# A chain of four convolution layers on one core: queues of the stores, steps of the division, layout of x2, place of the weight preparation

## The chip, the cores and the metric

The kernel runs on one core of a Trainium2 chip. Its engines are TensorE (PE, matrix products; PEld is its weight load), VectorE (DVE), ScalarE (ACT), GpSimd (POOL) and SyncE (SP, which here only issues DMAs). Each engine works through its own instructions in order and waits on semaphores where it needs another's result. Sixteen DMA engines carry the transfers, which are issued from SP's queue and from ACT's. The metric is the device time of one execution in microseconds (us), as the median of several runs.

## The reference

Four layers on x of 4 images, 128 x 128 pixels, 128 channels, all in float32. Before each layer stands a group normalisation over 32 groups of four channels (`_gn`), and each layer's output is added to its input.

```python
# layer 0: deformable convolution (offsets from a 1x1 product), relu
x = x + relu(deform_conv(gn(x), ...))
# layer 1: a scan over image rows; conv1d of width 9 along a row
def step(carry, row):
    new = row + relu(conv1d_same(carry, W));  return new, new
# layer 2: each pixel, the sum over its row and the sum over its column
x = x + (v @ Wself.T + (v.sum(2) @ Wm.T)[:, :, None] + (v.sum(1) @ Wk.T)[:, None]),  v = gn(x)
# layer 3: triangle multiplication
xn = layer_norm(gn(x))
left, right = (xn @ left_w) * sigmoid(xn @ lgate_w), (xn @ right_w) * sigmoid(xn @ rgate_w)
out = einsum('bkjd,bkid->bijd', left, right)
x = x + (layer_norm(out) * sigmoid(xn @ ogate_w)) @ to_out_w
```

(The biases and the gains of the norms are left out here; the kernel has them.)

## The kernel before

The kernel is one program with four stages one after the other.

`deform_layer` (layer 0) takes the first 3083 us and is not touched by the change. It leaves x1 in DRAM.

`last_weights` (L1158) and `message_weights` (L1225) prepare the weights of the last layers: the four projection matrices and the gate matrix are loaded (ACT's queue; the biases on SP's), scaled by the norm's gain, and brought into the form `wcat` by PE products of 512 and 128 columns, whose results go through two PSUM banks of their own and are copied by DVE. This stands between layer 0 and layer 1.

`scan_layer` (layer 1, L1011) goes row by row over all four images at once, 128 rows. SP loads four rows of x1 at a time (`x1rows`), PE transposes each row (`x1T_ps`), ACT applies the norm (`rowT`), and PE computes the convolution of the row before in two halves (`both_ps`, `own_ps`, three banks for the latter), which DVE adds up (`total`, `carry`). The rows of x2 are collected four at a time in `x2c`; DVE takes their statistics and their sums, and ACT's queue stores them to `x2T` in DRAM, split into a left and a right half of each row (two stores per image, L1148). A scheduler decides the order of the instructions in this stage.

`message_terms` computes the sums of layer 2 that are the same along a row or a column.

`last_layers` (L1289) does layers 2 and 3 image by image. Here the order on every engine is the one in which the program writes it (`manual_schedule`); generators are advanced step by step in a loop at the end of the function, so that the work of two images interleaves:

- `messages(b)`: 16 steps. SP loads 16 half rows of x2 (`x2c`, L1348), two steps ahead; PE multiplies (L1364); DVE adds `zc`, which POOL made, and writes X (L1369), an SBUF array of the whole image with the channels on the partitions; DVE takes two statistics (L1374).
- `scaled(b)`: 3 steps. The statistics become the norm's scale by a short chain DVE, PE (L1387), DVE, PE (L1398), ACT (`s`, L1400), DVE, PE (L1410). Ahead of `s` in the program stand eight stores of X to `x3T` in DRAM, 1 MB each, on SP's queue (L1395).
- `normed(b)`: 25 steps. PE centres X in tiles of eight columns (L1456); ACT squares (`sq`, L1462); ACT and DVE in turn write the centred tile back to X (L1467, L1469); for each group of two tiles PE sums the squares over the channels (L1490). Each group then starts a `divided` generator.
- `divided(b, j0, pv)`: ACT takes the square root (`std`, L1421). The 2048 values lie along one row, so they go through DRAM: SP stores them (L1424), loads them spread over the partitions (`rstd`, L1427), DVE takes the reciprocal (L1429), SP stores it (L1431) and loads it copied to all partitions (`rwide`, two loads of 256 KB for each half group, L1437), and X is multiplied by it (L1445), one of the two parts on DVE and one on POOL. Each of these lies one step behind the other, the multiplication two. The divisions that aren't finished when `normed` ends are advanced in the next stage.
- `multiplied(b, q)`: for each quarter q of the hidden channels 16 steps of projections (PE L1515, ACT sigmoid `sig` L1520, DVE product into T L1523), with the gates' product every second step (`gate`, stored to `gateT` from SP), then 8 steps of products over pixels (L1542). In the last quarter the messages of the next image run beside it.
- `given_out(b)`: 32 output columns of four, with six steps of lead for the statistics (L1567): layer norm (`u`, by ACT and POOL), transposes (L1601), `y` (ACT, then POOL times `gate`), and the products with x3 and the output weights (L1612, L1616); SP loads x3 and the gate and stores the output. It runs beside the next image's stages; for the last image it runs alone.

The tiles `std`, `rwide` and `sig` take turns in one set of four buffers (tag `half`); `gate` has three of its own; `x2c`, `zc` and `sq` share four (`wide`). A tile that takes a buffer waits until the last user of it is done.

## Time and profile before

| | |
|---|---|
| median of 3 runs | 5491.95 us (5491.25 to 5511.62) |
| profiled execution | 5500.92 us, its span 5499.1 us, mean granted clock 0.956 |
| PE busy | 4923.4 us, 90% of the span |
| DVE, ACT, POOL busy | 3263.9, 2492.0, 1269.4 us |
| layer 0 | to 3083 us |
| preparation of weights | 3083 to 3106.5 us |
| scan | 3106.5 to 3966.7 us |
| terms of the messages | to 3986.3 us |
| first image: first message product, first centring product, first projection | 3986.3, 4044.9, 4102.0 us |
| second image, the same | 4265.2, 4357.4, 4418.1 us |
| third image, the same | 4632.7, 4724.9, 4784.7 us |
| fourth image, the same | 4999.2, 5091.4, 5151.4 us |
| last output alone | 5390 to 5499.1 us |

Times within the span are counted from its start. A line of the timeline gives the start, the length, the engine ("q" for its queue of DMA issues), the line of the kernel, the operation, what it writes and reads, and in brackets how long the engine had been idle before it and what ended that. A line of the view of waits gives who waited for whom, how long in total, how often, and the longest in us. A line of the view by stage gives the stretch and its length, and for each engine its busy time and, in brackets, its number of instructions, in the order PE, PEld, DVE, ACT, POOL; then the granted clock of PE, the share of the DMA engines and what they moved in GB/s.

### The profile page before, as it was taken

To read this page: it belongs to the slowest core of one execution; us is meant where nothing else is said; L and a number is where in the kernel's file an instruction comes from. 1 tells how busy PE (TensorE), PEld (TensorE's weight loads), DVE (VectorE), ACT (ScalarE), POOL (GpSimd) and SP (SyncE) were. 2 spreads that over 40 slices of the span, in tenths; PEclk is the share of its full clock that TensorE was granted. 3 is DMA by queue.
4 is the path that set the end of the run, shared out by engine and by line. 5 is a ranking of instruction groups with operands and counts; after the bars stand their busy time and mean duration, and the time that the engine had idled before them with its cause. 6 is when DMAs were issued, how large, how long until landed. Compare 5 with 4: busy or idle time off the path is not lost. (4 is left out here: it accounts for less than half of the span.)

```text
span 5499.1 us, 163068 instructions
## 1 busy us (share of the span) xinstructions
PE 4923.4 (90%) x68902; PEld 4257.7 (77%) x68902; DVE 3263.9 (59%) x8405; ACT 2492.0 (45%) x5131; POOL 1269.4 (23%) x1161
## 2 busy tenths in 40 slices
PE   1898899999999998989999799999979789798897
PEld 1787788888888787878899699999838478486596
DVE  4676666666566656665555466666654655556445
ACT  1555454544554544545544133222224465564565
POOL 4222221210221201212000011111240343333424
PEclk9999999999998999999999899999989999899998
DMA  4776656665566765655544233333251544545436
GB/s 150 162 161 150 128 135 145 145 150 100 136 140 138 158 120 110 150 115 135 119 94 86 74 82 78 78 78 78 58 172 59 191 157 135 189 154 187 150 131 194
DMA packets 1390555, 710.69 MB, mean 129 GB/s; under 512 B 978765, under 2 KB 1245294, under 8 KB 1380598
## 3 DMA queue, kind: packets, MB, share of 16 engines
q1 hardware_dynamic: 1243538, 658.56, 47.6%
q10 hardware_dynamic: 146276, 41.60, 3.4%
q8 instruction: 545, 8.93, 0.7%
q14 instruction: 196, 1.61, 0.1%
HBM read 417.28 MB, written 282.55 MB: 127 GB/s over the span
## 5 line engine op out<-in xcount | busy, mean ns | idle before, releaser
L606 PE MATMUL conv_ps<-ring,wdef 128*128 128x192 f32 (+2 forms) x7632 | 1304.3, 320 | 7.1 <-DVE x1c L576 5.0
L514 DVE TENSOR_TENSOR m<-t_ps,tent 128x390 f32<-128x390 f32 x1548 | 806.7, 557 | 784.5 <-ACT tent L512 769.0
L606 PEld LDWEIGHTS conv_ps<-ring,wdef 128*128 128x128 f32 x7632 | 1150.0, 196 | 127.7 <-issue 64.8
L512 ACT COPY tent<-t_ps 128x390 f32<-128x390 f32 x1560 | 691.2, 488 | 654.6 <-PE t_ps L498 646.0
L498 PE MATMUL t_ps<-parts_of,spread 57*64 57x99 bf16 (+1 forms) x12384 | 743.1, 275 | 167.5 <-DVE m L514 146.8
L523 PE MATMUL v_ps<-m,pixels 60*64 60x108 f32 (+1 forms) x22704 | 811.6, 264 | 20.8 <-DVE m L514 8.7
L498 PEld LDWEIGHTS <-spread 57*64 57x64 bf16 x12480 | 578.8, 126 | 313.2 <-issue 265.8
L523 PEld LDWEIGHTS v_ps<-m,pixels 60*64 60x64 f32 x22704 | 672.0, 137 | 71.4 <-DVE m L514 21.3
L549 ACT COPY ring<-v_ps 128x432 f32<-128x432 f32 x1032 | 505.6, 525 | 452.1 <-PE v_ps L523 451.3
L420 POOL TENSOR_TENSOR off<-off,koff 72x512 f32<-72x512 f32 x128 | 162.9, 1273 | 1770.2 <-DVE off L417 1770.2
L1515 PEld LDWEIGHTS pair_ps<-wcat,X 128*128 128x128 f32 x4096 | 486.7, 196 | 79.5 <-issue 65.5
L1515 PE MATMUL pair_ps<-wcat,X 128*128 128x128 f32 x4096 | 498.0, 280 | 34.7 <-DVE T L1523 28.9
L1523 DVE TENSOR_TENSOR T<-pair_ps,sig 128x256 f32<-128x256 f32 x512 | 281.1, 592 | 389.0 <-ACT sig L1520 388.1
L1110 PEld LDWEIGHTS own_ps<-diff,wconv 128*128 128x128 f32 x4064 | 493.6, 191 | 13.1
L1110 PE MATMUL own_ps<-diff,wconv 128*128 128x128 f32 x4064 | 494.6, 273 | 0.0
L506 PE MATMUL t_ps<-parts_of,spread 57*64 57x130 bf16 x9288 | 455.1, 225 | 0.0
L1153 POOL TENSOR_TENSOR sum_h<-sum_h,x2c 128x512 f32<-128x512 f32 x128 | 162.7, 1271 | 1162.7 <-DVE x2c L1136 1162.7
L438 DVE SCALAR_TENSOR_TENSOR parts<-off,parts 72x512 bf16<-72x512 f32 x384 | 296.3, 772 | 152.5 <-ACT parts L430 146.8
L506 PEld LDWEIGHTS <-spread 57*64 57x64 bf16 x9312 | 319.3, 108 | 0.1
L1068 ACT ACTIVATE rowT<-x1T_ps,t_x,s_x 128x128 f32<-128x128 f32 x512 | 200.9, 573 | 248.6 <-PE x1T_ps L1064 232.0
L1520 ACT ACTIVATE sig<-pair_ps 128x512 f32<-128x512 f32 x256 | 151.8, 597 | 332.2 <-PE pair_ps L1515 190.4
L1099 PE MATMUL both_ps<-carry,wsum 128*128 128x128 f32 x2032 | 270.5, 275 | 6.0 <-DVE carry L1133 1.4
(197 smaller groups left out, 6736.9 us busy)
## 6 DMA issues: line engine op xcount, KB each, us to landing
pixels<-tab SPq DMA_DIRECT2D x688, 123.8 KB
parts_of<-off SPq DMA_DIRECT2D x1032, 55.7 KB
off<-parts SPq DMA_DIRECT2D x64, 891.0 KB
tab<-rows SPq DMA_DIRECT2D x384, 128.0 KB
xin<-in_x_dram SPq DMA_DIRECT2D x128, 256.0 KB
x<-x1c SPq DMA_DIRECT2D x32, 1024.0 KB
x1rows<-x SPq DMA_DIRECT2D x128, 256.0 KB
x2T<-x2c ACTq DMA_DIRECT2D x256, 128.0 KB
```

The costliest lines, as they stand in the source:

```text
L438: nc.vector.scalar_tensor_tensor(parts[:, NSPLIT + i, h : h + RO, 2 : S + 2], off, 0.0, part, ALU.is_gt, ALU.mult,)
L498: nc.tensor.matmul(tp[h : h + HALF, 0, 0:n].rearrange("p (r c) -> p r c", c=PADW)[:, :, i:PADW:RX], lhsT=spread[0:k, kx // 2, i, h : h + H ...
L506: nc.tensor.matmul(tp[h : h + HALF, 1, i * PADW : (i + 1) * PADW], lhsT=spread[HALF : HALF + k, kx // 2, first + i, h : h + HALF], rhs=src ...
L512: nc.scalar.copy(tent[:, 0:n], tp[:, 0, 0:n])
L514: nc.vector.tensor_tensor(m, *pair, ALU.mult)
L523: nc.tensor.matmul(to[p1 : p1 + HALF], lhsT=pix[p0 : p0 + LANES, xb, :], rhs=m[p0 : p0 + LANES, :, RX * xb : RX * xb + w], start=True, sto ...
L549: nc.scalar.copy(to, bodies[side])
L606: nc.tensor.matmul(pc[:, at : at + rows, x0:x1], lhsT=wdef[:, side, k, :], rhs=v[:, :, k if v.shape[2] == NK else kx, x0 + kx : x1 + kx], ...
L1099: nc.tensor.matmul(both, lhsT=wsum[:, j, :], rhs=old[h][:, 1, :, j : j + V], start=(j == 0), stop=(j == NJ - 1),)
L1110: nc.tensor.matmul(own[:, n], lhsT=wt[:, 2 * j + n, :], rhs=diffs[h][:, n, :, j : j + V], start=False, stop=(n == 1 and j == NJ - 1),)
L1515: nc.tensor.matmul(pj[:, j], lhsT=X[:, j0 + j, :], rhs=w.wcat[:, q * 4 * DQ : (q + 1) * 4 * DQ], start=True, stop=True,)
L1523: nc.vector.tensor_tensor(to, pj[:, :, e].rearrange("p j d -> p d j"), sig[:, :, e].rearrange("p j d -> p d j"), ALU.mult,)
```

## The change

- The preparation of the weights is called from within the scan, at row 8, and takes its PSUM banks from the scan's `own_ps`.
- x2T is laid out in whole rows: one store per image and four rows in place of two; a load of the messages takes half of each of 16 rows, in pieces of 256 bytes.
- The eight stores of x3T are issued from ACT's queue.
- `std` takes a buffer of the gates' three, `sig` and `rwide` have two each; both parts of the multiplication are on DVE; in `divided` there are two steps between the issue of a transfer of the std and its use, and one in place of two between the loads of `rwide` and the multiplication.
- `given_out` has seven steps of lead in place of six, and its steps are spread otherwise over the stages of the next image.

```diff
@@ scan_layer
+            if y == 2 * RB:
+                beside(ps_y, "own_ps")
...
-                    for n in range(2):
-                        nc.scalar.dma_start(
-                            x2T[b, :, n, y0 : y + 1, :], x2c[:, b, :, n * V : (n + 1) * V]
-                        )
+                    nc.scalar.dma_start(x2T[b, :, y0 : y + 1, :], x2c[:, b])
@@ last_weights
-            pw = ps_w.tile([P, 512], F32, name="prep_ps")
+            pw = psum.tile([P, 512], F32, name="prep_ps", tag=bank)
...
-            pb = ps_w.tile([P, 512], F32, name="prepb_ps")
+            pb = psum.tile([P, 512], F32, name="prepb_ps", tag=bank)
@@ messages
-                    nc.sync.dma_start(x2c, x2T[b, :, n, y0 : y0 + RB, :])
+                    nc.sync.dma_start(
+                        x2c, x2T[b, :, y0 : y0 + RB, n * V : (n + 1) * V]
+                    )
@@ scaled
-                nc.sync.dma_start(x3T[b, :, j0 : j0 + 16, :], X[:, j0 : j0 + 16, :])
+                nc.scalar.dma_start(x3T[b, :, j0 : j0 + 16, :], X[:, j0 : j0 + 16, :])
@@ divided
-            std = four.tile([P, 512], F32, name="std", tag="half")
+            std = three.tile([P, 512], F32, name="std", tag="gate")
             nc.scalar.activation(std, pv, AF.Sqrt, bias=c.eps)
...
             nc.sync.dma_start(stdT[b, 0, tokens].rearrange("(q e) -> q e", q=4), std[0:P:32])
             yield
+            yield
             rs = two.tile([P, 2 * JB], F32, name="rstd")
             nc.sync.dma_start(rs, stdT[b, 0, tokens].rearrange("(p e) -> p e", p=P))
             yield
+            yield
             nc.vector.reciprocal(rs, rs)
             yield
             nc.sync.dma_start(stdT[b, 1, tokens].rearrange("(p e) -> p e", p=P), rs)
+            yield
             yield
             for h in range(2):
                 rws = []
                 for j1 in (j0 + h * JB, j0 + h * JB + 4):
-                    rw = four.tile([P, 4 * S], F32, name="rwide", tag="half")
+                    rw = two.tile([P, 4 * S], F32, name="rwide")
...
                 yield
-                yield
-                for (j1, rw), engine in zip(rws, (nc.vector, nc.gpsimd)):
+                for j1, rw in rws:
                     flat = X[:, j1 : j1 + 4, :].rearrange("p j i -> p (j i)")
-                    engine.tensor_tensor(flat, flat, rw, ALU.mult)
+                    nc.vector.tensor_tensor(flat, flat, rw, ALU.mult)
@@ multiplied
-                sig = four.tile([P, JB, 2 * DQ], F32, name="sig", tag="half")
+                sig = two.tile([P, JB, 2 * DQ], F32, name="sig")
@@ given_out
-            for k in range(-6, NS_ + 1):
+            for k in range(-7, NS_ + 1):
...
-                if k + 6 < NS_:
-                    statistics(k + 6)
-                    if k + 7 in groups:
-                        scales(groups[k + 7], k + 7)
+                if k + 7 < NS_:
+                    statistics(k + 7)
+                    if k + 8 in groups:
+                        scales(groups[k + 8], k + 8)
@@ last_layers, the loop over images
-            n = 0
-            while step(msgs):
-                step(out_of, 2 if n < 2 else 1)
-                n += 1
-            for _ in scaled(b):
-                step(out_of)
+            step(out_of)
+            for n, _ in enumerate(msgs):
+                if n < 3:
+                    step(out_of)
+            for n, _ in enumerate(scaled(b)):
+                step(out_of, (2, 1, 1)[n])
             norm = normed(b)
             for n in range(25):
                 step(norm)
-                if n in (7, 15, 23):
+                if n in (4, 9, 14, 19, 24):
                     step(out_of)
@@ tile_preact_convs
-    x2T = dram.tile([B, P, 2, S, S // 2], F32, name="x2T")
+    x2T = dram.tile([B, P, S, S], F32, name="x2T")
...
-    w = last_weights(tc, c, wp, w3)
     with tc.tile_pool(name="l2", bufs=1) as l2:
-        w2 = message_weights(tc, l2, (wself_T, wm_T, wk_T))
-        counted = scan_layer(tc, c, l2, x1, w_conv, norms, x2T)
+        made = []
+
+        def weights(psum, bank):
+            made.append(last_weights(tc, c, wp, w3, psum, bank))
+            made.append(message_weights(tc, l2, (wself_T, wm_T, wk_T)))
+
+        counted = scan_layer(tc, c, l2, x1, w_conv, norms, x2T, weights)
+        w, w2 = made
```

More of the change, by code (lines that the diff above doesn't have):

```diff
@@ L1008, in deform_general, with scan_layer @@
                 nc.vector.tensor_copy(to, v)
-def scan_layer(tc, c, small, x1, w, norms, x2T):
+def scan_layer(tc, c, small, x1, w, norms, x2T, beside):
     nc = tc.nc
@@ L1155, in scan_layer, with last_weights @@
     return stats, sum_w, sum_h
-def last_weights(tc, c, wp, w3):
+def last_weights(tc, c, wp, w3, psum, bank):
     nc = tc.nc
@@ L1185, in last_weights @@
     w.gcols = slice(NQ * 4 * DQ, NP_)
-    with tc.tile_pool(name="l3prep", bufs=1) as prep, tc.tile_pool(
-        name="l3ps_w", bufs=2, space=PSUM
-    ) as ps_w:
+    with tc.tile_pool(name="l3prep", bufs=1) as prep:
         raw = prep.tile([P, NP_], F32, name="wraw")
```

## The prediction

> **What bounds the kernel now.** I read the page first, then the busy time by stage, then who waits for whom, then the timeline of the stages in which TensorE (PE) idles.
>
> ```profile
> span 5499.1 us, 163068 instructions
> ...
> PE 4923.4 (90%) x68902; PEld 4257.7 (77%) x68902; DVE 3263.9 (59%) x8405; ACT 2492.0 (45%) x5131; POOL 1269.4 (23%) x1161
> ```
>
> PE is busy 90% of the span, so a change that leaves the products alone can gain at most the 576 us in which PE idles. Only stages from 3083 us on are touched. The view by stage (busy us per engine, granted clock, DMA share, GB/s):
>
> ```profile
> 3083.00:3106.50 23.50, 4.51 (x8) 2.26 (x8) 4.96 (x16) 0.00 (x0) 0.00 (x0) 0.52 0.65 147
> 3106.50:3966.70 860.20, 854.06 (x7116) 834.03 (x7116) 567.87 (x1433) 257.64 (x766) 161.47 (x127) 1.00 0.31 76
> 4680.70:4709.10 28.40, 13.55 (x37) 6.62 (x36) 27.65 (x54) 8.42 (x16) 10.17 (x6) 0.83 0.80 282
> 4709.10:4725.00 15.90, 11.38 (x55) 10.09 (x56) 7.01 (x28) 9.54 (x19) 3.57 (x3) 0.71 0.97 379
> 4725.00:4784.70 59.70, 48.49 (x178) 18.94 (x177) 18.16 (x34) 37.70 (x48) 20.41 (x19) 0.90 0.38 116
> ```
>
> Row 1 is the preparation of weights between deformation and scan: PE does 4.5 us of work in 23.5. Row 2 is the scan: PE 99% busy, so nothing that relieves DVE, ACT or a queue there can gain. Rows 3 to 5 are the third image's last five message steps (DVE busy 27.7 of 28.4, so DVE bounds), `scaled` (PE waits on a chain, and the DMA engines are 97% busy) and `normed` (no engine full: PE 48.5 of 59.7). From the waits:
>
> ```profile
> POOL X L1445 <- DMA rwide<-stdT: 93.0, 36, 31.6
> ACT std L1421 <- POOL X L1445: 54.1, 14, 7.1
> ```
>
> and the third image's timeline:
>
> ```profile
> 4694.08 13.88 SPq L1395 DMA_DIRECT2D x3T<-X  x8
> ...
> 4761.44 0.69 ACT L1421 ACTIVATE std<-one_ps,eps 128x512 f32<-128x512 f32 x1 [5.08 <-POOL X L1445]
> ...
> 4770.64 1.92 PE L1490 MATMUL one_ps<-sq,mean 128*32 128x512 f32 x4 [8.84 <-ACT sq L1462]
> ...
> 4797.61 5.79 PE L1515 MATMUL pair_ps<-wcat,X 128*128 128x128 f32 x32 [4.99 <-DVE T L1523]
> ```
>
> `std`, `rwide` and `sig` share four buffers. ScalarE's `std` waits until a division (POOL, L1445) frees one; ACT's next squares stand behind it; PE's variance product waits 8.84 us for those, and the projections 4.99 us for a `sig` held the same way. What sets the pace is the division loop, seen undisturbed in the first image:
>
> ```profile
> 4079.86 0.79 SPq L1437 DMA_DIRECT2D rwide<-stdT  x2
> ...
> 4081.18 4.45 SPq L1437 DMA_DIRECT2D rwide<-stdT  x2
> ...
> 4084.02 1.27 POOL L1445 TENSOR_TENSOR X<-X,rwide 128x512 f32<-128x512 f32 x1 [1.97 <-PE one_ps L1490]
> ...
> 4088.42 1.27 POOL L1445 TENSOR_TENSOR X<-X,rwide 128x512 f32<-128x512 f32 x1 [1.23 <-DMA rwide<-stdT]
> 4088.52 0.79 SPq L1437 DMA_DIRECT2D rwide<-stdT  x2
> ```
>
> Two round trips of `rwide` per group of 16 columns, 4079.86 to 4088.52: 8.7 us a group, where PE and ACT alone take 4.7 (the first three `std` start at 4055.3, 4060.0, 4064.6).
>
> **The change, part by part.** Savings are counted against the profiled execution (span 5499.1, time 5500.9); the median of the runs, 5492.0, is 8.9 lower, and I take the same saving off it.
>
> *Start of the scan.* Its first transposes start at 3106.56, after the weights' copies (the idle before them ends with DVE `wcat`). Now the loads of x1 come first on SP, from 3089.4, where the first bias load was; four issues take 1.8 us. No row shows their landing; the nearest is the last weight load, issued 3096.54 and used by PE at 3101.0: 4.5 us. So PE starts near 3095.7: -10.9. The preparation moves into row 8 of the full scan: two products of 512 columns at 1.0 (two of that size take 1.98 us in the message stage) and two of 128 at 0.27 = 2.5 us of PE. They take `own_ps` banks, of which there are three; the instruction order puts a 2.27 us `sum_w` between two of the four copies on DVE, and PE's next `own_ps` is behind: between 0 and 5 us, I take 2. DVE's 2.5 us hide in its free third. Sum -6.4, bounds -3 and -10.
>
> *x2 in whole rows.* Four stores in place of eight per four rows, on an ACT that has 70% free beside a full PE: nothing, and about the same for the last stores, since PE idles there for DVE's statistics. The loads (L1348) now read 256 bytes at a time, 2048 pieces a load. Nearest row: ACT's queue, which carries the x2 stores in such pieces, took 3.4% of 16 engines for 146,276 packets, 20.4 ns each, so 2.6 us a load over 16 engines; as now laid out, 512 KB at the first image's 210 GB/s at share 0.64 (328 at full) take 1.6. So +1.0 a load. DVE paces these steps at 3.12 us and each load is issued two steps ahead: hidden, except for a few tenths at the start, where PE already waits for loads (0.7 to 1.9 us a step): +2 in the first image, +1 in each other. If every step waited: +14 and +3.
>
> *x3T stores from ACT.* SP no longer stands 13.9 us over them; the loads of `gate` and x3 behind no longer make PE wait (1.26 and 1.66 us, image 3). The eight issues, 0.3 to 0.85 us each on SP, now stand ahead of `u` and of `s` on ACT. The last four wait for the last X; DVE then needs 3.6 us to L1387 and 1.4 more to L1398 before `s`, and four issues at 0.55 plus `u` at 2.1 fit into 5.0. Cover gone, they cost up to 4. [...] I take nothing, because in the changed program's list of waits the stores wait for the DMA eight places earlier, which are those loads; the first image's first store waits for all of them. The same holds the other way: the first `rstd` load waits for the fifth store to land. Four stores after the last X are 4 MB, 12.8 us at 328 GB/s, down some 15 us after it; the first `std` comes 3.6 + 8.5 + 9 = 21 us after it: hidden by 6 us, and each us beyond that would delay the first division by one.
>
> *Steps of the output moved.* Before: 7 in the messages, 3 in `scaled`, 3 in `normed`, 26 in the projections; now 4, 4, 5, 27 with one more step of lead. DVE's message steps lose three statistics at 1.2: -3.6, and the loads' +1 makes -2.6. `scaled` now meets steps -3 to 0, of which PE works only in the last two: 3.6 us (the first image, with no steps: 4041.35 to 4044.94) + 1.1 + 1.1 of transposes + 1.7 of products + 1 waiting for the first y = 8.5 for 15.8: -7 (bounds -3, -9). The extra step in the projections costs a full 1.9.
>
> *Buffers and steps of the std.* `std` goes to the gates' three buffers, `sig` and `rwide` get two each, and both multiplications go to DVE at 0.68. ACT's waits for POOL are gone. What is late next is DVE: it stands in order at each multiplication until `rwide` lands, and its X (L1469) and T (L1523) are behind. Loop with two buffers: a pair lands about 4.1 us after the first issue, two multiplications, next issues as each buffer comes free: 4.0 to 4.5 a trip, two trips, 8.0 to 9.0 a group; I take 8.7. But PE may run a group ahead. From the first centring product: `std` at 9.0, then 7.0 where an output step stands between (4.7 + 2.3) and 4.7 where not; the first multiplication, three groups behind, at 27, the fifth at 27 + 4 x 8.7 = 62. PE reaches the projections at 53 (before 59.7), does two steps, and waits for T behind that fifth multiplication until 62.5; before, it resumed at 4797.6 - 4725.0 = 72.7. So -10, with two more output steps inside. Later waits of 1 us: -1.
>
> *Sum.* Images 2 to 4: -2.6 - 7 - 10 + 1.9 - 1 = -18.7 each, -56. First image, no output steps: the third projection step resumes at 58 for 66.4 (4111.35), half of its later waits of 1.9 and 1.2 gone, loads +2: -8. Last output: one more statistics step of 1.2 ahead of the first y: +1.5; its 3 us stalls (PE for `u`) stay, since the square root stands in the same place in ACT's order. With the start: -69. Median 5492 - 69 = **5423**.
>
> **Rivals.**
> *PE runs through (0.16).* The trips shorten to about 3.3 us, since less stands on SP. For: the single trip 4085.3 to 4088.4 took 3.1. Against: both trips carry two loads. Then `normed` and start give -15, `scaled` -9, messages -4, an image -29; the first -13; start -9: 5383.
> *The loop stays long (0.12).* SP's queue also holds output stores, gate loads that wait for POOL, and `std` stores, and two buffers leave no slack: 12 us a group. The fifth multiplication comes at 75, -10 becomes +3, an image -6, the first +2: 5471.
> *Slower, by the same loop (0.10).* DVE must do all multiplications in order, so past 12.7 us a group the T behind the seventh and eighth groups is late too: at 14, +11 in the start of the projections and +9 further on, an image +11, the first +15: about 5535. For: one step, about 2 us, between load and use, where there were two. Against: the present trips.
> *The change does not do what it says:* the stores of x3 gain nothing from their own queue because the DMA engines are 97% busy in `scaled`; its -7 becomes -3: 5435, inside the forecast.
>
> **How the numbers follow.** Forecast 0.62, its own range 5387 to 5460 from the bounds above. A measurement of this kernel tells about 0.5% from no change, 5464.5 to 5519.4. Faster: 0.61 of the forecast, 0.16, and 0.04 of the long loop: 0.81; same: 0.10 (mostly the long loop); slower 0.09. The range reaches into the run-through case below and over the long loop above: 5375 to 5482.
>
> **What would show it.** Right: no `std` waiting for POOL; PE's wait for squares in `normed` under 2 us; L1364 to L1387 about 25 us in image 3, then 8 to 9 to the first centring product; DVE waiting for `rwide` some 2 us twice a group, and PE waiting for T once per image by 2 to 4 us; the scan's first transposes 11 us earlier after 3083. Wrong: multiplications of successive groups 11 us apart or more; PE waiting for x2 loads in every message step; `s` in `scaled` ended by ACT rather than PE.

## The result, and the profile after

The changed kernel takes 5459.34 us, the median of five runs (5454.3 to 5471.3), where the kernel before takes 5492.53 us over five (5491.25 to 5511.62). The ratio is 0.9935, with a 95% interval of 0.9915 to 0.9956: faster by 0.65%. The forecast was 5423 us (range 5375 to 5482), a gain of 69 us; 33 us came.

The page of the changed kernel, from an execution of 5471.3 us, the longest of its five runs:

```profile
span 5469.6 us, 162747 instructions
...
PE 4908.4 (90%) x68902; PEld 4255.7 (78%) x68902; DVE 3298.1 (60%) x8469; ACT 2491.3 (46%) x5131; POOL 1192.2 (22%) x1097
```

PE is still busy 90% of the span. The view by stage, with the stages and columns in the order of the prediction (start of the scan, scan, last message steps of the third image, `scaled`, `normed`):

```profile
3078.10:3090.90 12.80, 0.02 (x1) 0.05 (x1) 3.13 (x12) 0.00 (x0) 0.00 (x0) 0.50 0.42 114
3090.90:3945.80 854.90, 852.75 (x7124) 836.67 (x7124) 578.00 (x1436) 259.93 (x766) 161.41 (x127) 1.00 0.26 80
4657.60:4686.00 28.40, 13.31 (x28) 4.81 (x27) 26.26 (x44) 2.23 (x4) 9.24 (x5) 0.82 0.84 252
4686.00:4695.80 9.80, 7.79 (x26) 5.52 (x27) 7.58 (x31) 7.27 (x15) 2.54 (x2) 0.50 1.02 422
4695.80:4758.40 62.60, 51.72 (x210) 22.87 (x209) 27.77 (x52) 45.12 (x63) 12.59 (x12) 0.92 0.45 144
```

The start takes 12.8 us where it took 23.5 us, and `scaled` 9.8 for 15.9. The third row begins at the end of the last product of T (4657.6); from that point the messages took 32.1 us before (4677.0 to 4709.1), so that they are 3.8 us shorter, although the prediction's row, which begins later, has the same 28.4 us. The scan is 5.3 us shorter, which the forecast did not have. `normed` is *longer*, 62.6 for 59.7, where a good part of the gain was to come from. The timeline of the changed kernel at the end of that stage (in brackets the idle time and what ended it):

```profile
4739.38 1.34 DVE L1446 TENSOR_TENSOR X<-X,rwide 128x512 f32<-128x512 f32 x2 [2.50 <-DMA rwide<-stdT]
...
4743.31 1.29 DVE L1446 TENSOR_TENSOR X<-X,rwide 128x512 f32<-128x512 f32 x2 [1.39 <-DMA rwide<-stdT]
...
4747.44 0.31 ACT L1585 ACTIVATE rs<-rs,eps 128x16 f32<-128x16 f32 x1 [9.76 <-DVE rs L1582]
...
4751.26 1.92 PE L1491 MATMUL one_ps<-sq,mean 128*32 128x512 f32 x4 [7.29 <-ACT sq L1463]
...
4758.86 1.32 DVE L1446 TENSOR_TENSOR X<-X,rwide 128x512 f32<-128x512 f32 x2 [2.40 <-DMA rwide<-stdT]
...
4763.05 1.28 DVE L1446 TENSOR_TENSOR X<-X,rwide 128x512 f32<-128x512 f32 x2
4764.25 1.10 DVE L1524 TENSOR_TENSOR T<-pair_ps,sig 128x256 f32<-128x256 f32 x2
```

No `std` waits for POOL any more. In its place ACT stands 9.76 us at `rs`, the square root of an *output* step that lies among the normalisation's tiles. It waits for DVE, which takes that step's statistics in order behind two pairs of multiplications, each held up by its `rwide`. ACT's next squares stand behind the root, and PE waits 7.29 us for them.

Stage by stage, the two profiled executions set against the forecast, in us. A row with two numbers gives the length of the stage before and after the change; the scan is counted here to the first product behind it, 8.1 us after its own last one:

| step of the forecast | forecast | measured |
|---|---|---|
| layer 0, same code (end of its last product at 3066.4, 3061.5) | 0 | -4.9 |
| from there to the scan's first transposes: 40.2, 29.4 | -10.9 | -10.8 |
| the scan with the preparation in it: 868.2, 863.0 | +4.5 | -5.2 |
| first image, messages: 55.1, 69.9 | +2 | +14.9 |
| first image, `normed` and first quarter of the projections | -10 | -5.2 |
| images 2 to 4, messages | -7.8 | -10.8 |
| images 2 to 4, `scaled` | -21 | -18.6 |
| images 2 to 4, first centring product to third projection step | -30 | -7.9 |
| images 2 to 4, rest of the projections | +2.7 | +10.5 |
| last output: 102.1, 110.6 | +1.5 | +8.5 |
| sum | -69 | -29.5 (span) |

The rows are differences of points in time read from the two traces. The rest of the projections holds the extra output step in the last quarter (+5.9, forecast +5.7).

### The profile page after: what moved, and what is told of

It is laid out like the page before. It is cut to its first block, busy times and chain, and to the rows that moved or that the text cites. A ratio compares the mean times of both kernels' runs of the same rounds, so it can differ in the third digit from the quotient of the medians.

```text
span 5469.6 us, 162747 instructions
## 1 busy us (share of the span) xinstructions
PE 4908.4 (90%) x68902; PEld 4255.7 (78%) x68902; DVE 3298.1 (60%) x8469; ACT 2491.3 (46%) x5131; POOL 1192.2 (22%) x1097
```

## The experiments

My theory after the result had four parts: in the first image the loads of x2 are late (small pieces, or the stores beside them); in images 2 to 4 two limits hold `normed`, the output's square root on ACT and the loop of `rwide`; the granted clock, 0.75 over 82.1 us of the last output, makes that longer; and the scan gained from something in the stores of x2. Each run below edits the changed kernel. "Ratio" is that of its time to the kernel before, with a 95% interval; lengths of stages are those of its one profiled execution.

**x2 laid out as before.**

```diff
-                    nc.scalar.dma_start(x2T[b, :, y0 : y + 1, :], x2c[:, b])
+                    for n in range(2):
+                        nc.scalar.dma_start(
+                            x2T[b, :, n, y0 : y + 1, :], x2c[:, b, :, n * V : (n + 1) * V]
+                        )
...
-                    nc.sync.dma_start(
-                        x2c, x2T[b, :, y0 : y0 + RB, n * V : (n + 1) * V]
-                    )
+                    nc.sync.dma_start(x2c, x2T[b, :, n, y0 : y0 + RB, :])
...
```

> The changed kernel with x2 laid out as before: eight stores of half rows per four rows, loads of 4 KB in one piece per partition. Theory (the 256-byte pieces make the first image's message steps wait for their loads): the stretch from the first message product to the first product of the scale falls from 69.9 us to about 55 us, and PE's wait for x2c there from 26 us to about 5 us; the time falls by 10 to 15 us. Rival (the loads are late for another reason, such as what the scan leaves in the queues): the stretch stays near 70 us. Second question, the scan, which became 0.09 us a row shorter: if the whole-row stores did that, a row goes from 6.66 us back to 6.75 us and the scan costs 11 us more, so that the two parts nearly cancel; if not, a row stays at 6.66 us.

Measured: 5463.18 us (5450.21 to 5476.04; ratio to the kernel before 0.9942, interval 0.9916 to 0.9968), no different from the changed kernel. The first image's messages take 60.3 us, not 55, and the scan 874.4 us, 11.4 more. So the layout gave 11 us in the scan and took 10 in the first image, as the second question supposed; but 5 us of the longer messages stay without any small piece (60.3 us, and 55.1 before the change).

**First image in whole rows.**

```diff
+            if b == 0:
+                RB, V = JB, S
-            todo = [(n, y0) for n in range(2) for y0 in range(0, S, RB)]
+            todo = [(n, y0) for n in range(S // V) for y0 in range(0, S, RB)]
...
```

(The products and the statistics follow the new shape of a step.)

> The changed kernel, but the first image's messages take eight whole rows of x2 a step in place of half of sixteen rows; its loads are then in one piece of 4 KB per partition, and everything else stays. Theory (256-byte pieces): the first image's message stretch falls from 69.9 us to about 55 us, the time by about 15 us, 0.3%. Rival (another cause): the stretch stays near 70 us and the time is the same.

Measured: 5454.7 us (5442.9 to 5460.0; ratio 0.9926, 0.9902 to 0.9949). The messages take 56.2 us, as expected, but the median falls by only 4.6 us, and the next stage shows a part of the reason: the step from there to the first centring product takes 7.4 us in place of 3.6. With whole rows all eight stores of X wait for the last X, and the timeline of this kernel has them on ACT's queue ahead of the norm's root `s`:

```profile
4016.47 8.31 ACTq L1399 DMA_DIRECT2D x3T<-X  x8
...
4024.83 0.26 ACT L1404 ACTIVATE s<-one_ps,eps 128x1 f32<-128x1 f32 x1 [62.08 <-issue]
...
4025.93 0.58 PE L1414 MATMUL one_ps<-shift,center 128*128 128x1 f32 x2 [4.91 <-DVE shift L1411]
```

This is the cover whose loss the prediction priced at up to 4 us; it cost 3.8.

**Weights ahead of the scan again.**

```diff
-            if y == 2 * RB:
-                beside(ps_y, "own_ps")
...
+    w = last_weights(tc, c, wp, w3, None, None)
     with tc.tile_pool(name="l2", bufs=1) as l2:
```

> The changed kernel with the weights of the last layers prepared ahead of the scan again. Theory (the move is worth what the start of the scan shows): the first transposes of the scan come about 15 us later, about 3 us of that are won back in the first rows and 3 us where the preparation stood, so the time rises by about 10 us. If the shorter rows of the scan (6.66 us in place of 6.75 us) come from the other order that the scheduler found with the preparation inside, they go back to 6.75 us and the time rises by about 20 us in all; if they come from the stores in whole rows, they stay.

Measured: 5473.73 us (5457.38 to 5478.31; ratio 0.9957, 0.9941 to 0.9973). From the end of layer 0 to the first transposes 39.0 us pass in place of 29.4; the scan takes 856.6 us in place of 863.0. The move is worth 9.6 - 6.4 = 3.2 us in the traces, the lower bound of the forecast for it and less than expected here. (The medians differ by 14 us; these stages do not account for the rest.) Rows stay short, so the preparation's place did not make them so.

**Stores of x3 on SP again.**

```diff
-                nc.scalar.dma_start(x3T[b, :, j0 : j0 + 16, :], X[:, j0 : j0 + 16, :])
+                nc.sync.dma_start(x3T[b, :, j0 : j0 + 16, :], X[:, j0 : j0 + 16, :])
```

> The changed kernel with the eight stores of X issued from SP's queue again. Theory (SP standing over the stores kept the output's loads back and PE with them): images 2 to 4 need about 14 to 16 us from the first product of the scale to the first centring product in place of 9.8 us, together 12 to 18 us more. Rival (the six us came from having the output's first steps there, which have little work for PE, not from the queue): the stretch stays near 10 us and the time within 4 us.

Measured: 5473.55 us (5454.41 to 5500.19; ratio 0.9961, 0.9947 to 0.9975). `scaled` takes 15.0, 15.1 and 15.0 us in images 2 to 4, in place of 9.7 to 9.9. The timeline of this kernel in the third image shows who is late:

```profile
4689.58 0.47 PE L1613 MATMUL one_ps<-ident,x 128*128 128x128 f32 x1 [4.19 <-DMA x<-x3T]
...
4690.33 2.63 POOL L1605 TENSOR_TENSOR y<-y,gate 128x512 f32<-128x512 f32 x2 [20.90 <-DMA gate<-gateT]
...
4691.65 0.79 PE L1617 MATMUL one_ps<-outw,y 128*128 128x128 f32 x2 [1.59 <-POOL y L1605]
```

That is the queue, as predicted. The surprise is the first image: its messages take 59.5 us here, against 69.9 with the stores on ACT. The timeline of the changed kernel:

```profile
3994.83 3.11 ACTq L1394 DMA_DIRECT2D x3T<-X  x4
...
3996.78 9.73 SPq L1345 DMA_DIRECT2D x2c<-x2T  x2
3996.97 1.96 PE L1363 MATMUL pair_ps<-x2c,ws 128*128 128x512 f32 x4 [0.22 <-DMA x2c<-x2T]
...
4010.86 2.04 PE L1363 MATMUL pair_ps<-x2c,ws 128*128 128x512 f32 x2 [11.94 <-DMA x2c<-x2T]
```

and of this one:

```profile
3998.14 5.37 PE L1363 MATMUL pair_ps<-x2c,ws 128*128 128x512 f32 x8 [3.28 <-DMA x2c<-x2T]
...
4005.05 1.96 PE L1363 MATMUL pair_ps<-x2c,ws 128*128 128x512 f32 x4 [1.55 <-DMA x2c<-x2T]
...
4010.31 2.60 SPq L1394 DMA_DIRECT2D x3T<-X  x3
```

After eight of the sixteen steps half the columns of X are done, and four stores of 1 MB start from ACT's queue, between two loads of x2. The load issued next, at 3996.78, serves PE only at 4010.86, after an 11.94 us wait. From SP the stores go out behind all loads. Of the 14.9 us, 10.4 go with these stores (69.9 - 59.5), and the 4.4 that are left with the small pieces (59.5 - 55.1). The two are not a plain sum: without small pieces the stores cost 5.2 us (60.3 - 55.1), and beside the stores the small pieces cost 9.6 (69.9 - 60.3). The stretch itself takes 67.9 to 74.2 us in the profiles of the eight other runs that leave both as in the changed kernel.

**Every second multiplication on POOL again.**

```diff
-                for j1, rw in rws:
+                for (j1, rw), engine in zip(rws, (nc.vector, nc.gpsimd)):
                     flat = X[:, j1 : j1 + 4, :].rearrange("p j i -> p (j i)")
-                    nc.vector.tensor_tensor(flat, flat, rw, ALU.mult)
+                    engine.tensor_tensor(flat, flat, rw, ALU.mult)
```

> The changed kernel with the second of each two multiplications by the std on POOL again. Theory (in images 2 to 4 DVE, in order behind multiplications that wait for their transfers, is what keeps the last tiles of the normalisation back): the stretch from the first centring product to the first projection falls from 62.5 us to about 55 to 58 us in images 2 to 4, and the wait between the sixth and the seventh std from 18 us to 10 to 13 us; the time falls by 10 to 20 us. Rival (the transfers and their two buffers set the loop, whichever engine multiplies): groups stay 8 to 10 us apart, the stretch stays within 2 us, and as POOL takes 1.27 us for what DVE does in 0.68 us, the time rises by up to 5 us.

Measured: 5484.47 us (5462.98 to 5502.65; ratio 0.9974, 0.9959 to 0.9989): slower than the changed kernel, and the rival's side. The stretch to the projections of images 2 to 4 changes by -1.4, +3.0 and +3.1 us, and the sixth and the seventh `std` still start 19 to 21 us apart. DVE's load was not the limit. The rival had allowed for 5 us more, and 25 came: groups of the first image come 9.4 us apart in place of 8.1, which fits a slower multiplication (in the kernel before 1.27 us on POOL, 0.68 on DVE) that holds the two buffers longer. Both multiplications on DVE are a good part of the change.

**The output's square root one step later.**

```diff
                     if k + 8 in groups:
-                        scales(groups[k + 8], k + 8)
+                        pending.append((k, scales(groups[k + 8], k + 8)))
...
                     outs[k] = x3
+                while pending and (k < 0 or pending[0][0] < k):
+                    roots(*pending.pop(0)[1])
```

(`scales` keeps the first four DVE instructions; `roots` holds ACT's root and the two that follow on DVE.)

> The changed kernel with the output's square root (ACT) and what follows it on DVE moved one step of the output later, behind that step's copy; its results are needed two steps after the statistics, so that one step of slack is left. Theory: in the normalisation of images 2 to 4, ACT no longer waits 9.8 us for DVE's statistics, the 18 us between the sixth and the seventh std become about 8 us, and the stretch to the first projection falls from 62.5 us to about 53 us; in the last output PE no longer idles 3.3 us in every fourth step, four steps take about 10.5 us in place of 13.7 us. Together 25 to 50 us less. Rival (the normalisation is held by the transfers of the std, and the last output by DVE): the stretch stays at 60 us or more, four steps stay above 12 us, and the time falls by less than 10 us.

Measured: 5445.89 us (5428.81 to 5452.47; ratio 0.9895, 0.9864 to 0.9925). In the third image PE reaches the projections 54.2 us after the first centring product, in place of 62.6; but then it waits for T, and the third projection step comes at 68.0 us, in place of 68.8. The last output's four steps take 11.3 us on average (67.6 us for 24). So the theory holds for the last output (10.5 was expected), and for `normed` half: the root was late, and behind it stood the loop of the division.

**Lead of six in the output.**

```diff
-            for k in range(-7, NS_ + 1):
+            for k in range(-6, NS_ + 1):
...
-                if k + 7 < NS_:
-                    statistics(k + 7)
+                if k + 6 < NS_:
+                    statistics(k + 6)
```

(and `k + 7` in place of `k + 8` for the scales)

> The changed kernel with six steps of lead in the output as before, at the same places of the loop. Theory A (the lead of seven makes PE's wait in every fourth step of the last output longer, 3.3 us in place of 3.0 us, and the clock drops after each): four steps of the last output take 12.2 us again in place of 13.7 us, the time falls by 8 to 10 us. Theory B (the lead has nothing to do with it; the cycle of 13.65 us is one that the dropping clock keeps up by itself, and the kernel before started in another phase): four steps still take 13.6 us, and only the one statistics step of 1.2 us at the start is saved.

Measured: 5471.31 us (5459.38 to 5473.23; ratio 0.9948, 0.9929 to 0.9966). In the profile 24 steps of the last output take 75.1 us in place of 82.1, four of them, from wait to wait, 11.4 to 13.4 (in the changed kernel 13.65 to 13.74), at a granted clock of 0.84 over the stretch in place of 0.75; PE's waits there are 3.0 us or less. Theory A holds for the stretch. The time does not follow, since the images lose what it gains (`scaled` is 2.0 to 2.8 us longer in images 2 to 4; 1.8 us ahead of the changed kernel at the end of the scan, it is 5.5 us behind at the end of the fourth image).

**Four buffers for `rwide` and `sig` together.**

```diff
-                    rw = two.tile([P, 4 * S], F32, name="rwide")
+                    rw = four.tile([P, 4 * S], F32, name="rwide", tag="half")
...
-                sig = two.tile([P, JB, 2 * DQ], F32, name="sig")
+                sig = four.tile([P, JB, 2 * DQ], F32, name="sig", tag="half")
```

> The changed kernel with rwide and sig taking turns in one set of four buffers, so that in the normalisation rwide has four in place of two. Theory (the loop of the division is set by two trips one after the other, because the third load waits for a buffer): groups come 5 to 6 us apart in the first image in place of 8.2 us, PE's wait for T at the start of its projections (15.1 us for two steps) falls to about 7 us, and images 2 to 4 gain 3 to 6 us each; together 15 to 25 us less. Rival (the order of the waits on SP and DVE sets the loop, not the buffers): groups stay 8 us apart and the time is the same.

Measured: 5421.98 us (5416.23 to 5426.81; ratio 0.9858, 0.9831 to 0.9885), 37 us under the changed kernel. In the first image DVE's multiplications of successive groups start at 4062.4, 4068.9, 4074.7, 4080.6 and 4086.3, 6.0 us apart; with two buffers at 4062.9, 4071.3, 4079.1, 4087.1 and 4095.3, 8.1 us apart. The first two projection steps take 8.5 us in place of 15.1. The gain is larger than expected, because the later projection steps of each image had waited for the same loop: they get 3 to 7 us shorter per image. The same amount of SBUF in one set of four was worth more here than in two sets of two; that the two users hardly overlap in time would explain it.

**x2 in whole rows, in two stores of two rows.**

```diff
-                    nc.scalar.dma_start(x2T[b, :, y0 : y + 1, :], x2c[:, b])
+                    for n in range(0, RB, 2):
+                        nc.scalar.dma_start(
+                            x2T[b, :, y0 + n : y0 + n + 2, :], x2c[:, b, n : n + 2])
```

> The changed kernel with x2 stored in whole rows, but in two stores of two rows each per image and four rows: as many issues on ACT's queue as before the change, and twice the piece. Theory A (a row of the scan got 0.09 us shorter because ACT issues four stores in place of eight, and its work comes earlier): a row takes 6.75 us again, the scan 874 us, the time rises by about 11 us. Theory B (the size of the pieces did it): a row stays at 6.66 us, the scan at 863 us and the time is the same.

Measured: 5461.69 us (5451.39 to 5464.88; ratio 0.9929, 0.9905 to 0.9952); the scan takes 862.9 us. The number of issues is not it. PE's timeline shows what differs. With half rows (the first of these experiments):

```profile
3330.56 1.03 PE L1064 MATMUL x1T_ps<-ident,x1rows 128*128 128x128 f32 x8
3332.08 1.13 PE L1101 MATMUL both_ps<-carry,wsum 128*128 128x128 f32 x8 [0.49 <-DVE carry L1131]
```

and in the changed kernel:

```profile
3346.23 0.60 PE L1064 MATMUL x1T_ps<-ident,x1rows 128*128 128x128 f32 x4
3346.66 1.06 PE L1101 MATMUL both_ps<-carry,wsum 128*128 128x128 f32 x8
```

With half rows, the scheduler that orders the scan had put the transposes of two rows together 31 times, and PE waits for DVE's `carry` behind them. From such a pair to PE's next product 1.17 us pass in most cases, where two single rows take 0.87; the pairs account for 9.5 of the 11.4 us. With whole rows, in one store or two, PE transposes one row at a time but for one pair; the kernel before had 31 pairs too. So the order of the instructions differs with the form of the store. What in that form moves the scheduler was not tried, nor was the same order kept with the other store.

**Later root and four buffers together.** The two edits shown above, in one kernel:

```diff
-                        scales(groups[k + 8], k + 8)
+                        pending.append((k, scales(groups[k + 8], k + 8)))
...
-                    rw = two.tile([P, 4 * S], F32, name="rwide")
+                    rw = four.tile([P, 4 * S], F32, name="rwide", tag="half")
```

> The changed kernel with the later square root of the output and rwide in the set of four with sig, both. Theory (they are two separate limits of the normalisation: ACT waits at the square root, and T waits for the loop of the division; either alone uncovers the other): from the first centring product to the third projection step images 2 to 4 take about 60 us in place of 68.8 us (the later root alone 68 us, the four buffers alone 65 us), the first image gains 14 us as with four buffers alone, the last output 20 us; the time is about 5390 us, less than the sum of the two gains off 5459 us would leave were they one and the same. Rival (the same wait in two places): no more than the four buffers alone plus the last output, about 5403 us.

Measured: 5392.0 us (5384.94 to 5393.7; ratio 0.9809, 0.9787 to 0.9831), as expected. The view by stage, from the first centring product to the third projection step of the third image, for the changed kernel:

```profile
4695.80:4764.60 68.80, 57.92 (x260) 28.55 (x259) 32.80 (x63) 50.80 (x72) 14.98 (x15) 0.92 0.46 148
```

with the later root alone:

```profile
4705.50:4773.50 68.00, 58.49 (x261) 28.99 (x259) 33.98 (x65) 51.40 (x74) 15.03 (x15) 0.93 0.49 151
```

with the four buffers alone:

```profile
4668.30:4733.40 65.10, 57.86 (x259) 28.58 (x259) 33.35 (x63) 50.78 (x72) 15.07 (x15) 0.95 0.52 162
```

and with both:

```profile
4658.60:4719.80 61.20, 56.72 (x261) 28.84 (x260) 34.46 (x65) 51.25 (x73) 15.02 (x15) 0.97 0.55 172
```

The second column is the length. The edits save 0.8 and 3.7 us alone and 7.6 together: two limits in series, each covering the other. Over images 2 to 4 they save 5.2 and 13.7 us alone and 28.3 together.

**All of it: both, and the first image in whole rows with its stores of X on SP.**

```diff
-                nc.scalar.dma_start(x3T[b, :, j0 : j0 + 16, :], X[:, j0 : j0 + 16, :])
+                (nc.sync if b == 0 else nc.scalar).dma_start(
+                    x3T[b, :, j0 : j0 + 16, :], X[:, j0 : j0 + 16, :]
+                )
```

(The other edits are those shown above.)

> As the run with both, and the first image's x2 loaded in eight whole rows a step and its X stored from SP's queue. Theory (the first image's message stretch holds 4 us of small pieces and 10 us of stores that share the DMA engines with the loads): the stretch falls from 69.9 us to about 55 us with the 3.6 us to the first centring product kept, and the time is about 14 us under the run with both, near 5376 us. Rival (the stores then delay something later in the first image): less than 8 us under it.

Measured: 5367.62 us (5359.98 to 5381.12; ratio 0.977, 0.9748 to 0.9792): 2.3% faster than the kernel before, 92 us under the changed one and 24 us under the run with both. The first image's messages take 55.3 us and the step after them 3.6, as before the change; this explains 14 of the 24. In the profiled executions layer 0 ended 11.0 us earlier than in that of the run with both, which says how little a difference of ten microseconds between two executions means.

**PE kept busy in the last output's waits.**

```diff
+                    if alone and k + 7 in groups:
+                        spare = single((P, 4, P))
+                        for j in range(20):
+                            nc.tensor.matmul(
+                                spare[:, j % 4], lhsT=c.ident, rhs=c.ident, start=True, stop=True)
                     pt = single((P, 4, P))
```

> The changed kernel with 20 products of 128 columns of the identity by itself, which nobody reads, put on PE in the last output ahead of the transposes for which it waits 3.3 us in every fourth step: about 2.2 us of work in that wait, and nothing else is moved. Theory (the cycle of 13.7 us is long because the granted clock drops after each such wait, to 0.75 over the stretch): the clock stays above 0.95, four steps take about 11.6 us (8.3 us of PE's work at full clock and the wait of 3.3 us), 24 steps about 70 us in place of 82.1 us, the time 10 to 13 us less, though PE has more to do. Rival (the chain of statistics, square root and u sets the cycle, and the clock only follows): 24 steps take 82 us or more, the time is the same.

What the products are to fill is seen in the changed kernel's timeline:

```profile
5407.08 1.11 PE L1602 MATMUL one_ps<-ident,u 128*128 128x128 f32 x4 [3.30 <-ACT u L1632]
5407.99 0.42 PE L1613 MATMUL one_ps<-ident,x 128*128 128x128 f32 x1
...
5413.14 0.27 PE L1613 MATMUL one_ps<-ident,x 128*128 128x128 f32 x1
```

For 5.6 us after the wait the same products take 0.42 us each, then 0.27 again; the granted clock is 0.50 from 5407.08 to 5412.70 us, and 0.97 in the 4.3 us behind. Measured over 24 steps of the last output, in the view by stage, for the kernel before:

```profile
5412.40:5486.40 74.00, 54.45 (x387) 50.84 (x386) 52.26 (x152) 45.45 (x78) 47.97 (x75) 0.88 0.81 258
```

the changed kernel:

```profile
5375.00:5457.10 82.10, 61.94 (x387) 59.67 (x386) 53.54 (x148) 45.05 (x78) 49.50 (x73) 0.75 0.73 232
```

this one:

```profile
5373.80:5449.10 75.30, 74.07 (x627) 69.94 (x626) 50.93 (x148) 45.87 (x79) 50.53 (x73) 1.00 0.79 253
```

and the one with the later root:

```profile
5369.40:5437.00 67.60, 51.01 (x387) 42.64 (x386) 50.42 (x148) 45.83 (x79) 47.76 (x74) 1.00 0.91 279
```

With 240 more instructions on PE (each of the 120 products is two in the profile) the stretch is 6.8 us shorter, the clock 1.00, and the same products take 0.27 us; with the clock at 0.50 after each wait they had taken 0.42 in the changed kernel, so it was the clock that slowed them. It is 75 us and not the expected 70, since the filling was sized wrong:

```profile
5413.18 4.63 PE L1603 MATMUL one_ps<-ident 128*128 128x128 f32 x40
```

Twenty products hold PE for 4.5 us to the start of the next transposes, not 2.2, which is more than the wait of 3.3 us that they fill; PE is busy 74.07 of 75.3 us. The time, 5469.21 us (5462.09 to 5478.45; ratio 0.9958, 0.9944 to 0.9972), shows no gain over the changed kernel: a gain of 7 us isn't to be seen where layer 0 alone moves by more, and I can't claim one.

## Why the prediction was right and where it was wrong

**Start of the scan: right, with a smaller sum.** The first transposes came 10.8 us nearer to the end of layer 0, forecast 10.9. What it costs inside was 6.4 us and not 4.5 (856.6 to 863.0 us), and the gain 9.6 where only the weights' place differs, so -3.2 for -6.4, near the upper bound of -3.

**x2 in whole rows: wrong twice, in opposite directions.** "Nothing" for the stores missed the order of the scan, worth 11 us. For the loads the prediction took "+2 in the first image", "hidden, except for a few tenths at the start". The small pieces cost 4.4 with the stores out of the way and 9.6 beside them. PE waited for x2 11 times in this stage, 26.2 us in all, where five waits of 5.4 us in all had been; waiting in every step had been named as a sign that the prediction would be wrong.

**x3T stores from ACT: right for `scaled`, wrong for the first image.** With the queue alone turned back, `scaled` is 5.2 to 5.4 us longer in each of images 2 to 4: the rival that these stores gain nothing from their own queue is refuted. The step that failed is the "nothing" taken for loads of x2 that run beside the stores: "the stores wait for the DMA eight places earlier, which are those loads". The first four stores need only the first half of X's columns, and in the first image they went out between two loads (from 3994.83 us), not behind them. 10.4 us of the first image went with it (69.9 us, and 59.5 with the stores on SP); no run separates what a second queue does to the loads from the plain load of these 4 MB on the same engines. Images 2 to 4 lost nothing: 28.3 us of their last messages are 28.3 with the stores on SP as well. But the reason is not the one given. In the third image of the changed kernel:

```profile
4674.97 1.95 PE L1363 MATMUL pair_ps<-x2c,ws 128*128 128x512 f32 x4 [1.60 <-DMA x2c<-x2T]
...
4677.57 0.31 ACT L1585 ACTIVATE rs<-rs,eps 128x16 f32<-128x16 f32 x1 [17.72 <-DVE rs L1582]
4677.57 9.92 ACTq L1394 DMA_DIRECT2D x3T<-X  x8
```

ACT works in order and stood 17.72 us at the root of an output step, so that the stores went out only when PE had used the last load of x2. The first image has no output step beside it, and nothing held its stores back. For images 2 to 4 the "nothing" was right by luck.

**Steps of the output moved: right in sum.** Messages -10.8 (forecast -7.8), `scaled` -18.6 (-21), the extra step +5.9 (+5.7). In `scaled` the shares were off: with the stores back on SP 15.0 to 15.1 us are left of the 15.8 to 16.1 before, so that of the 6.2 us an image at most 1.1 come without the change of queue, where the rival had supposed 3.

**Buffers and steps of the std: the largest miss, -8 for -30.** The loop itself was predicted well: 8.1 us a group in the first image (forecast 8.7), and in the third image the first multiplication of the fifth group at 63.1 us after the first centring product (forecast 62). Two steps of the argument failed. "PE reaches the projections at 53": it did so at 62.6, since an output step put into `normed` has its square root on ACT, in order behind DVE; PE then waited 7.29 us for the squares, where under 2 us had been named as a sign of being right. With the root moved, it comes at 54.2. And "waits for T behind that fifth multiplication until 62.5": it is the second half of the fifth group that stands ahead of the second T, at 67.3, so that the third projection step comes at 68.8. I had counted one round trip of `rwide` where the group has two. The second error covered the first, which is why either edit alone showed little there, and both together brought the third step to 59.8 to 61.2 us, where the sum had supposed 62.5. The same loop held the later projections up, where -1 had been taken. One line had been read too simply: the prediction put PE's 4.99 us before the third step down to a `sig` held by POOL. In the kernel before, that `sig` ran at 4792.18, and T followed 3.7 us after it was done, because DVE, in order, stood at another division's `rstd`:

```profile
4796.29 0.25 DVE L1429 RECIPROCAL rstd<-rstd 128x16 f32<-128x16 f32 x1 [3.60 <-DMA rstd<-stdT]
4796.46 1.01 DVE L1523 TENSOR_TENSOR T<-pair_ps,sig 128x256 f32<-128x256 f32 x2
```

**Last output: wrong, +8.5 for +1.5.** The 3 us stalls stayed, as predicted, but they grew to 3.3 us and the clock over the stretch fell from 0.88 to 0.75. What made them grow is read from the traces only: the chain in the wait holds one of the products of y with the gate, which in the last image, whose output runs alone, are on DVE and not on POOL; in the changed kernel it takes 0.94 us on average while POOL works (30 of 32) and 0.69 when POOL is idle. Before the change POOL was idle there, because its u waited for the same root; with one step more of lead it works on. First the kernel before, then the changed one:

```profile
5428.43 0.67 DVE L1604 TENSOR_TENSOR y<-y,gate 128x512 f32<-128x512 f32 x1
...
5431.90 0.66 PE L1601 MATMUL one_ps<-ident,u 128*128 128x128 f32 x4 [3.01 <-ACT u L1631]
```

```profile
5403.31 0.97 DVE L1605 TENSOR_TENSOR y<-y,gate 128x512 f32<-128x512 f32 x1
```

The wait of 3.30 us behind it is the one shown above, at 5407.08. That the slow cycle goes with the longer lead is shown by the run with six; that this product is the link was only argued.

**The sum.** 4.9 us of the 29.5 between the two profiled executions are layer 0, which the change doesn't touch. That 5459 us lies within the forecast's range of 5375 to 5482 us is in part luck: the scan's order gave 11 us that nobody had forecast, and the range was wide enough for half of the gain to be missing. Without the two losses that are the change's own doing and no part of its aim (first image 14.9, last output 8.5) and with both limits of `normed` lifted, the kernel goes to 5367.62 us, below the forecast of 5423. Not all of that is the forecast's own: it did not have the scan's 11 us, and it left the last output's wait in place, which the later root removes. (A slip in the first rival: its -29 us an image leaves out the 1.9 us of the extra output step; 5383 us should be 5389.)

## What to carry to other kernels

Count the waits of an in-order engine for *all* that stands on it: a step of other work placed among a chain's tiles brings its own cross-engine round trip with it (here ACT stood 9.76 us at one root), and it is as late as the latest engine that it touches. When a stage has two limits in series, lift both before judging either; alone, each looks smaller than it is (0.8 and 3.7 us in the third image here, together 7.6). The stores moved to a queue of their own no longer started behind the loads (in the first image at 3994.8 us, between two of them, where from SP's queue they came at 4010.3, behind all), so ask of such a store when its data first become ready, what stands ahead of it on its new engine, and which loads are still under way then.

## What the runs showed of the hardware

- **In the last output a slow cycle went with a low clock.** In the changed kernel a wait of 3.3 us every fourth step is followed by 5.6 us of transposes and products at 0.42 us in place of 0.27, then by some at 0.27 and by the next wait; four steps take 13.65 to 13.74 us from wait to wait. The granted clock is 0.50 over such 5.6 us (5407.08 to 5412.70) and 0.75 over 24 steps. The cycle is seen in the profile of every run with seven steps of lead and the root in its old place, except the filled one; two of them (stores on SP, two stores of two rows) had first run four-step groups of 11.1 to 12.8 us from wait to wait, and then fell into it and stayed. With waits of 3.0 us or less (the kernel before, the lead of six) four steps vary between 11.4 and 13.4 us, at a clock of 0.88 and 0.84 over 24 steps. What keeps the slow cycle at its length was not shown; no run here varies its phase alone.
- **Multiplications on DVE took longer while POOL worked.** In the kernel before, 32 of DVE's multiplications of X by `rwide` ran while POOL was idle and took 0.68 us; the other 32 took 1.10 us on average. Three of these took 4.08 to 4.09 us, one in each of images 2 to 4, and each of the three ended 0.55 to 0.56 us after the last of four instructions that POOL ran without a pause. In the changed kernel, where POOL has none of these multiplications, the longest of 128 takes 1.28 us. No run varies POOL's work alone.
- **The same code of layer 0 varies by 23 us.** Its last product ended between 3049.8 us (the run with half rows) and 3073.1 us (the run with the later root) in the profiled executions, though nothing before it differs. Differences below 10 us between these kernels are read from the stages of a trace, not from the times.
